# Conditional residual adapter on one core: W1 fetched by id for seventeen batches instead of nine, without the early copy of W1

## The chip, the cores and the metric

The kernel runs on one core of one Trainium2 chip. The metric is the device time of one execution in microseconds (us); of several executions the median is given. A core has five engines that run their own instruction streams in order: TensorE (PE, whose weight loads the profile lists apart as PEld), VectorE (DVE), ScalarE (ACT), GpSimd (POOL) and SyncE (SP), which in this kernel only issues transfers. An instruction starts when the one before it on its engine allows it and the semaphores that it waits for have come.

## The reference: what is computed

There are 128 batches; each has x[b] of 128 rows by 512 columns (256 KB) and an id 0 to 8 that picks one of ten sets of weights.

```
w1 = W1[ids]; w2 = W2[ids]                       # 512x128 and 128x512 for each batch
h = relu(x @ w1 + b1[ids])                       # 128 x 128
y = x + (h @ w2 + b2[ids])                       # 128 x 512
n = (y - mean(y)) * rsqrt(var(y) + 1e-5)         # over the 512 columns
out = x + n * gamma[ids] + beta[ids]
```

All tensors are float32. W1 and W2 of all ten ids are 2560 KB each, x and out are 32 MB each.

## The kernel before, in words

**Per batch.** Each batch goes through the same steps, one batch behind the other on every engine:

- PE: `transpose_x` (line 260, four transposes of x into `pxT`), `down` (line 283, four products of x transposed with the batch's W1 into `ph`, listed as eight passes), `up` (line 300, one product with W2 into `py`, listed as two passes; for batches 0, 1, 126 and 127 a product at line 299 puts b2 there first).
- ACT: `copy_xT` (line 264) copies the transposed x from PSUM, `relu` (line 291), `stage_w1` (line 251) copies the 256 KB of the batch's W1 from the table that holds all ten into a small buffer `w1s`, `square` (line 340) sums squares, and two short steps for mean and deviation.
- POOL: `add_b2` (line 270, `r` = x + b2) and `add_beta` (line 277, `o` = x + beta). For some batches DVE adds b2 instead (line 310).
- DVE: `residual` (line 317), `scale` (line 383), three short steps for 1/deviation, `finish` (line 392, writes the result into `o`).
- SP: `load_x` (line 71, four batches or 1024 KB at a time), `load_part` (line 89, two batches or 512 KB), and `store` (line 396, two batches or 512 KB of `o`).

The function `keep` ties every instruction to the one before it on its engine, so that the order of each engine, SP's queue too, is the order in which the program writes it. `x` has four buffers of four batches; `o` has five buffers of two batches; `w1s` has five buffers of one batch; `py` has five and `pxT` and `ph` one PSUM buffer each. A buffer is filled anew when its last readers are done.

**W1 in the beginning.** For batches 0 to 8 SP loads the batch's own W1 from HBM by its id (`load_first`, line 162, 256 KB; the id is in a register that `lid` at line 144 loads, four ids at a time). Batches 9 to 29 are staged by ACT from `w1e`, a copy of all ten W1 that two loads of 1280 KB bring (`load_early`, line 170). Batches from 30 on are staged from `w1`, the usual copy with its rows in another order, which four loads of 640 KB bring (`load_w1`, line 104) in loop turns 16, 18, 20 and 22. `w1` has 512-byte pieces in HBM; `w1e` and the loads by id have 2 KB pieces, and `transpose_x` takes the columns of x with a stride of four for batches below `EARLY`.

**Opening and loop.** The opening (lines 522 to 561) spreads the rows of beta, gamma and b2 over 128 partitions (`spread` by PE and ACT, `shuffle_rows` at line 236 by DVE) among the first five turns of x; `spin` (line 511) issues idle products. Then a loop over i runs `transpose_x(i)`, `down(i-1)`, `copy_xT(i)`, `relu(i-1)`, `stage_w1(i+1)`, `up(i-2)` and, for b = i - 3, the steps on POOL and DVE; the store of a pair comes when its second batch is finished, first in turn i = 7. The last batches have an order of their own (`tail`).

Of the kernel before, what the change touches and what calls it, by code (L numbers as in the profile page):

```python
# [8 lines left out]
FP = mybir.dt.float32  # L9
# [4 lines left out]
ET = mybir.EngineType  # L14
PSUM = bass.MemoryType.PSUM

P = 128
G = 4
EPS = 1e-5
FIRST = 9  # L20
EARLY = 30
LATE = 12
U = 2


# [1 line left out]
def cond_resid_kernel(ctx: ExitStack, tc: tile.TileContext, x, itok, W1, b1, W2, b2, gamma, beta, out):  # L27
# [8 lines left out]
    nc = tc.nc  # L36
    B, S, H = x.shape
    L, _, A = W1.shape
    KC = H // P
    NG = B // G  # L40
# [5 lines left out]
    def keep(ins):  # L46

        engine = ins.ins.engine
        if engine in last:
            tc.add_manual_dep(ins.ins, last[engine], behind, reason="kept order")  # L50
        last[engine] = ins.ins.name
        return ins

    const = ctx.enter_context(tc.tile_pool(name="const", bufs=1))
    xp = ctx.enter_context(tc.tile_pool(name="xp", bufs=4))
    rp = ctx.enter_context(tc.tile_pool(name="rp", bufs=4))
    op = ctx.enter_context(tc.tile_pool(name="op", bufs=5))
    tp = ctx.enter_context(tc.tile_pool(name="tp", bufs=2))
    wp = ctx.enter_context(tc.tile_pool(name="wp", bufs=5))
    st = ctx.enter_context(tc.tile_pool(name="st", bufs=6))  # L60
    p_x = ctx.enter_context(tc.tile_pool(name="p_x", bufs=1, space=PSUM))
    p_h = ctx.enter_context(tc.tile_pool(name="p_h", bufs=1, space=PSUM))
# [3 lines left out]
    xs = {}  # L66
    E = B - 5

    def load_x(g):
        t = xp.tile([P, G, H], FP, tag="x", name=f"x_{g}")  # L70
        keep(nc.sync.dma_start(out=t, in_=x[g * G : (g + 1) * G].rearrange("b s h -> s b h")))
        xs[g] = t
# [6 lines left out]
    rows = rp.tile([P, H], FP, tag="r", name="rows")  # L79
    b1r = const.tile([L, A], FP, name="b1r")  # L80
    w1 = const.tile([P, L, KC, A], FP, name="w1")
    w1e = const.tile([P, L, KC, A], FP, name="w1e")
    w2 = const.tile([P, L * H], FP, name="w2")
    x_0 = xp.tile([P, G, H], FP, tag="x", name="x_0")
    xs[0] = x_0
# [1 line left out]
    def load_part(lo, hi, engine=nc.sync):  # L87
        dst = xs[lo // G][:, lo % G : lo % G + hi - lo, :]
        keep(engine.dma_start(out=dst, in_=x[lo:hi].rearrange("b s h -> s b h")))  # L89
# [12 lines left out]
    def load_w1(k):  # L102
        keep(
            nc.sync.dma_start(out=w1[:, :, k, :], in_=W1[:, k * P : (k + 1) * P, :].rearrange("l p a -> p l a"))
        )
# [35 lines left out]
    def lid(b, engine):  # L141
        g = b // G
        if (g, engine) not in lids:
            loads, vals = nc.values_load_multi_w_load_instructions(  # L144
                lang[0:1, g * G : (g + 1) * G],
                engines=[engine],
                min_val=0,
                max_val=L - 1,
                skip_runtime_bounds_check_because="clamped on the chip to 0..L-1 above",
            )  # L150
            for ins in loads:
                keep(ins)
            lids[g, engine] = vals
        return lids[g, engine][b % G]
# [4 lines left out]
    def load_first(b):  # L159
        w1s[b] = wp.tile([P, KC, A], FP, tag="w1s", name=f"w1s_{b}")  # L160
        src = W1[bass.ds(lid(b, ET.SP), 1)].rearrange("o (p k) a -> p (o k a)", k=KC)
        keep(nc.sync.dma_start(out=w1s[b].rearrange("p k a -> p (k a)"), in_=src))  # L162
# [2 lines left out]
        dst = w2[:, lo * H : hi * H].rearrange("p (l h) -> p l h", l=hi - lo)  # L165
        keep(nc.sync.dma_start(out=dst, in_=W2[lo:hi].rearrange("l a h -> a l h")))

    def load_early(lo, hi):
        dst = w1e[:, lo:hi].rearrange("p l k a -> p l (k a)")
        keep(nc.sync.dma_start(out=dst, in_=W1[lo:hi].rearrange("l (p k) a -> p l (k a)", k=KC)))  # L170

    load_w2(0, 3)
    load_first(0)
    load_first(1)
# [10 lines left out]
    load_first(7)  # L185
    xs[2] = xp.tile([P, G, H], FP, tag="x", name="x_2")
    load_part(8, 10)
    load_early(0, 5)
    load_first(8)
    load_early(5, L)  # L190
    load_part(10, 12)

    def upper(lo):

# [19 lines left out]
    def spread(r, copier):  # L214
        t = (beta_b, gamma_b, b2_b)[r // L]
        row = p_y.tile([P, H], FP, tag="y", name=f"row_{r}")
        pick_r = pick[:, r : r + 1].to_broadcast([96, P])
        keep(nc.tensor.matmul(row, lhsT=pick_r, rhs=parts[:96, :], start=True, stop=True))
        dst = t[:, r % L * H : (r % L + 1) * H]
        if copier is nc.scalar:  # L220
            keep(nc.scalar.copy(dst, row))
        else:
            keep(nc.vector.tensor_copy(dst, row))
# [9 lines left out]
    def shuffle_rows(lo, hi):  # L233
        for r in range(lo, hi):
            t = (beta_b, gamma_b, b2_b)[r // L]
            keep(nc.vector.stream_shuffle(t[:, r % L * H : (r % L + 1) * H], fours[0], [r] * 32))  # L236
# [10 lines left out]

    def stage_w1(b):
        w1s[b] = wp.tile([P, KC, A], FP, tag="w1s", name=f"w1s_{b}")
        src = (w1e if b < EARLY else w1).rearrange("p l k a -> p (l k a)")[:, bass.ds(lid(b, ET.Activation) * (KC * A), KC * A)]  # L250
        keep(nc.scalar.copy(w1s[b].rearrange("p k a -> p (k a)"), src))  # L251

    def transpose_x(b):
        pxs[b] = p_x.tile([P, KC, P], FP, tag="xT", name=f"pxT_{b}")
        for k in range(KC):
            if b < EARLY:
                cols = xb(b).rearrange("s (p k) -> s k p", k=KC)[:, k, :]
            else:
                cols = xb(b)[:, k * P : (k + 1) * P]
            keep(nc.tensor.transpose(pxs[b][:, k, :], cols, ident))  # L260

    def copy_xT(b):
        xT[b] = tp.tile([P, KC, P], FP, tag="xT", name=f"xT_{b}")
        keep(nc.scalar.copy(xT[b], pxs.pop(b)))  # L264

    def add_b2(b):
        if not b2_by_matmul(b) and not b2_by_vector(b):
            rs[b] = rp.tile([P, H], FP, tag="r", name=f"r_{b}")
            v = lid(b, ET.Pool)
            keep(nc.gpsimd.tensor_tensor(rs[b], xb(b), b2_b[:, bass.ds(v * H, H)], ALU.add))  # L270
# [8 lines left out]
    def down(b):  # L279
        phs[b] = p_h.tile([P, P], FP, tag="h", name=f"ph_{b}")  # L280
        for k in range(KC):
            keep(
                nc.tensor.matmul(  # L283
                    phs[b], lhsT=w1s[b][:, k, :], rhs=xT[b][:, k, :], start=(k == 0), stop=(k == KC - 1)
                )
            )
        del xT[b], w1s[b]

    def relu(b):
        hT[b] = tp.tile([P, P], FP, tag="hT", name=f"hT_{b}", bufs=6)  # L290
        keep(nc.scalar.activation(hT[b], phs.pop(b), AF.Relu, bias=b1T[:, bass.ds(lid(b, ET.Activation), 1)]))  # L291
# [107 lines left out]
    def on(b):  # L399
        return 0 <= b < B  # L400
# [125 lines left out]
    x_turn(0)  # L526
    transpose_b1()
    spread(11, nc.scalar)
    shuffle_rows(0, 10)
    x_turn(1)  # L530
    spread(12, nc.scalar)
# [28 lines left out]
    x_turn(4)  # L560
    up(1)

    for i in range(3, B + U):
        b = i - U - 1
        if b > G and b % G == 2 and b // G + 3 < NG:
            load_x(b // G + 3)
        if i == 5:
            load_x(3)
        if i in (16, 18, 20, 22):
            load_w1((i - 16) // 2)  # L570
        if i > 4 and on(i):
            transpose_x(i)
        if b <= E:
            add_b2(b + 2)
            if 4 <= b + 2 <= E:
                add_beta(b + 2)
        if i > 4 and on(i - 1):
            down(i - 1)
        if i > 4 and on(i):
            copy_xT(i)  # L580
        if i > 4 and on(i - 1):
            relu(i - 1)
        if i + 1 >= LATE and on(i + 1):
            stage_w1(i + 1)
        if i > 3 and on(i - U):
            up(i - U)


        g, half = divmod(b, 2)
        p = g - 1  # L590
        mine, old = 0 <= p < B // 2, 0 <= p - 1 < B // 2
        if b == E:
            add_b2(b + 3)
            add_beta(b + 1)
            add_b2(b + 4)
            for n in range(b + 2, B):
                add_beta(n)
        if b > E:
            tail(b)
        elif half == 0:  # L600
            if on(b):
                vector_b2(b)
                residual(b)
                square(b)
            if mine:
                scale(2 * p)
                rstd(p, 1)
            if old:
                finish(2 * p - 1)
                store(p - 1)  # L610
        else:
            if on(b):
                vector_b2(b)
            if mine:
                rstd(p, 2)
            if on(b):
                residual(b)
                square(b)
            if mine:
                rstd(p, 3)  # L620
                scale(2 * p + 1)
            if mine:
                finish(2 * p)
        if 0 <= g and b <= E and half == 1:
            scalar_means(g)
            deviation(g)
        if FIRST <= i + 1 < LATE:
            stage_w1(i + 1)

        for n, engine in ((i + 3, ET.Activation), (i - U + 3, ET.PE), (b + 1, ET.DVE), (b + 6, ET.Pool)):  # L630
            if on(n):
                lid(n, engine)

# [36 lines left out]
```

## Time and profile before

| what | value |
| --- | --- |
| median of three runs | 306.7 us (306.4 to 306.74) |
| the profiled execution's own time | 306.72 us |
| its span in the profile | 305.0 us |
| PE busy | 292.6 us (96%) |
| DVE busy | 294.4 us (97%) |
| POOL busy | 285.0 us (93%) |
| ACT busy | 282.8 us (93%) |
| moved by DMA | 77.85 MB, mean 255 GB/s |

The span is the time from the first to the last recorded event; 1.7 us of the execution's time lie around it. A busy figure is an average over the opening, the loop and the end, and a matmul's or a POOL instruction's listed length overlaps the next one's, so the distance from one start to the next is the better price of an instruction.

### The profile page before, as it was taken

How to read it: one execution, taken by the hardware profiler on the slowest of the kernel's cores; microseconds unless marked ns; L12 is line 12 of the kernel's file. 1: busy time of each engine (PE TensorE's matmuls, PEld its weight loads, DVE VectorE, ACT ScalarE, POOL GpSimd, SP SyncE). 2: the span in 40 equal slices, each digit the busy share in tenths (PEclk: the TensorE clock that was granted, in tenths of full speed). 3: DMA queues.
4: the chain of work that ended last, by engine and by line, in shares of the span. 5: the costliest groups of instructions: out<-in, count | busy, mean ns of one | idle time of the engine just before them, and what ended most of it. 6: DMA issues, size and time to landing. Idle time of an engine off the chain costs nothing.

```text
span 305.0 us, 6995 instructions
## 1 busy us (share of the span) xinstructions
PE 292.6 (96%) x1821; PEld 220.0 (72%) x1821; DVE 294.4 (97%) x784; ACT 282.8 (93%) x779; POOL 285.0 (93%) x240
## 2 busy tenths in 40 slices
PE   7999899999999999999999999999999999999980
PEld 3858587877777777777777777777777777777740
DVE  5989799999999999999999999999999999999995
ACT  4967899999999999999999999999999999999982
POOL 1199599999999999999999999999999999999995
PEclk9999999999999999999999999999999999999996
DMA  7999996998578766766876666777766766882244
GB/s 233 388 388 386 397 318 187 380 368 315 213 270 277 230 207 224 250 250 222 275 269 214 219 217 253 249 241 275 252 220 205 242 233 234 277 275 103 112 170 172
DMA packets 44057, 77.85 MB, mean 255 GB/s; under 512 B 1993, under 2 KB 7892, under 8 KB 44018
## 3 DMA queue, kind: packets, MB, share of 16 engines
q1 hardware_dynamic: 43382, 76.84, 73.1%
q10 hardware_dynamic: 636, 0.57, 0.6%
q8 instruction: 15, 0.25, 0.3%
q14 instruction: 24, 0.20, 0.2%
HBM read 43.85 MB, written 33.55 MB: 254 GB/s over the span
## 4 chain that ended last, share of the span: by engine, by line
PE 59%; POOL 15%; DMA 8%; issue 8%; DVE 7%; SPq 1%; ACT 1%; POOLq 0%; DVEq 0%; ACTq 0%
PE ph L283 24%; PE py L300 23%; PE pxT L260 12%; POOL o L277 8%; POOL r L270 6%; DMA w1e<-in_L_cond_W_dram 4%; DMA w1s<-in_L_cond_W_dram 3%; DVE py L383 2%; DVE py L317 2%; DVE o L392 1%; DVE py L310 1%; SPq L162 1%; SPq L89 0%; SPq L144 0%; ACT n L439 0%
## 5 line engine op out<-in xcount | busy, mean ns | idle before, releaser
L277 POOL TENSOR_TENSOR o<-x,beta_b 128x512 f32<-128x512 f32 x128 | 172.3, 1381 | 15.3 <-DVE beta_b L236 12.7
L283 PE MATMUL ph<-xT,w1s 128*128 128x128 f32 x1024 | 135.2, 275 | 0.0
L270 POOL TENSOR_TENSOR r<-x,b_b 128x512 f32<-128x512 f32 x97 | 134.1, 1384 | 0.6 <-DMA x<-in_x_dram 0.6
L300 PE MATMUL py<-w,hT 128*128 x256 | 131.3, 595 | 0.0
L283 PEld LDWEIGHTS ph<-xT,w1s 128*128 128x128 f32 x1024 | 125.1, 192 | 1.0 <-ACT hT L291 0.5
L260 PEld LDWEIGHTS pxT<-ident,x 128*128 128x128 f32 x512 | 68.2, 155 | 66.7 <-issue 48.6
L383 DVE SCALAR_TENSOR_TENSOR py<-py,nmean,gamma_b 128x512 f32<-128x512 f32 x126 | 94.8, 752 | 0.0
L392 DVE SCALAR_TENSOR_TENSOR o<-py,rstd,o 128x512 f32<-128x512 f32 x122 | 91.0, 746 | 0.0
L340 ACT ACTIVATE sq<-py,sum 128x512 f32<-128x512 f32 x124 | 85.8, 692 | 0.6 <-DVE py L317 0.6
L260 PE MATMUL pxT<-ident,x 128*128 128x128 f32 x512 | 78.7, 277 | 1.3 <-ACT hT L291 1.3
L264 ACT COPY xT<-pxT 128x512 f32<-128x512 f32 x128 | 74.7, 583 | 3.4 <-PE pxT L260 3.3
L317 DVE SCALAR_TENSOR_TENSOR py<-py,r 128x512 f32<-128x512 f32 x97 | 66.9, 689 | 1.9 <-PE py L300 1.7
L251 ACT COPY w1s<-w 128x512 f32 x98 | 60.0, 613 | 0.0
L291 ACT ACTIVATE hT<-ph,b1T 128x128 f32<-128x128 f32 x128 | 46.9, 367 | 7.0 <-PE ph L283 1.7
L300 PEld LDWEIGHTS py<-w,hT 128*128 128x128 f32 x256 | 39.1, 192 | 1.4 <-issue 0.7
L340 ACT ACTIVATION_READ_ACCUMULATOR sq<-py,sum 128x1 f32 x124 | 25.1, 203 | 0.0
L317 DVE SCALAR_TENSOR_TENSOR py<-py,x 128x512 f32<-128x512 f32 x31 | 21.7, 699 | 1.1 <-PE py L300 0.8
L310 DVE TENSOR_TENSOR py<-py,b_b 128x512 f32<-128x512 f32 x27 | 18.7, 691 | 0.1
L350 ACT ACTIVATE root<-ssq,eps 128x2 f32<-128x2 f32 x62 | 16.5, 265 | 0.0
L251 ACT COPY w1s<-w1e 128x512 f32 x21 | 12.8, 612 | 1.6 <-DMA w1e<-in_L_cond_W_dram 1.6
L317 DVE DVE_READ_ACCUMULATOR py<-py,r 128x1 f32 x97 | 13.5, 139 | 0.0
L331 ACT ACTIVATE nmean<-sum 128x2 f32<-128x2 f32 x62 | 12.3, 198 | 0.0
(58 smaller groups left out, 92.1 us busy)
## 6 DMA issues: line engine op xcount, KB each, us to landing
out_dram<-o SPq DMA_DIRECT2D x61, 512.0 KB, 3.4
x<-in_x_dram SPq DMA_DIRECT2D x29, 1024.0 KB, 6.2
x<-in_x_dram SPq DMA_DIRECT2D x6, 512.0 KB, 8.8
w1e<-in_L_cond_W_dram SPq DMA_DIRECT2D x2, 1280.0 KB, 12.5
w<-in_L_cond_W_dram SPq DMA_DIRECT2D x4, 640.0 KB
w1s<-in_L_cond_W_dram SPq DMA_DIRECT2D x9, 256.0 KB, 8.5
w<-in_L_cond_W_dram SPq DMA_DIRECT2D x1, 1792.0 KB, 10.0
w<-in_L_cond_W_dram SPq DMA_DIRECT2D x1, 768.0 KB, 5.3
```

The costliest lines, as they stand in the source:

```text
L251: keep(nc.scalar.copy(w1s[b].rearrange("p k a -> p (k a)"), src))
L260: keep(nc.tensor.transpose(pxs[b][:, k, :], cols, ident))
L264: keep(nc.scalar.copy(xT[b], pxs.pop(b)))
L270: keep(nc.gpsimd.tensor_tensor(rs[b], xb(b), b2_b[:, bass.ds(v * H, H)], ALU.add))
L277: keep(nc.gpsimd.tensor_tensor(os[g][:, j, :], xb(b), beta_b[:, bass.ds(v * H, H)], ALU.add))
L283: nc.tensor.matmul(phs[b], lhsT=w1s[b][:, k, :], rhs=xT[b][:, k, :], start=(k == 0), stop=(k == KC - 1))
L291: keep(nc.scalar.activation(hT[b], phs.pop(b), AF.Relu, bias=b1T[:, bass.ds(lid(b, ET.Activation), 1)]))
L300: keep(nc.tensor.matmul(ys[b], lhsT=hT[b], rhs=w2[:, bass.ds(v * H, H)], start=not m, stop=True))
L317: nc.vector.scalar_tensor_tensor(ys[b], ys[b], 1.0, r, ALU.mult, ALU.add, accum_out=col(sums, b))
L340: nc.scalar.activation(sq, ys[b], AF.Square, bias=col(sums, b), scale=-float(H), accum_out=col(ssqs, b))
L383: nc.vector.scalar_tensor_tensor(ys[b], ys[b], col(nmeans, b), gamma_b[:, bass.ds(v * H, H)], ALU.add, ALU.mult)
L392: nc.vector.scalar_tensor_tensor(o, ys.pop(b), rstds[g][:, j : j + 1], o, ALU.mult, ALU.add)
```

## The change

The early copy `w1e` and its two loads are gone, and with them ACT's staging for batches 9 to 16. Batches 9 to 16 get their W1 by id as batches 0 to 8 do; ACT stages from `w1` from batch 17 on. The four loads of `w1` and the loads of x for batches 12 to 19 are written into the list ahead of the loop, between the loads by id; so every store stands behind all of these on SP's queue. `o` has eight buffers instead of five, `w1s` seven instead of five. `transpose_x` uses the stride of four up to batch 16 instead of 29. PE loads the ids of batches 0 to 7 into registers ahead of the turn of batch 1 instead of at `up(0)` and in the loop. The loop is written anew around the variable `turned`; the order on each engine that results is the old one, but that `stage_w1` always follows `relu`.

```
-FIRST = 9
-EARLY = 30
-LATE = 12
+FIRST = 17
+EARLY = 17
+LATE = 17
...
-    op = ctx.enter_context(tc.tile_pool(name="op", bufs=5))
+    op = ctx.enter_context(tc.tile_pool(name="op", bufs=8))
...
-    wp = ctx.enter_context(tc.tile_pool(name="wp", bufs=5))
+    wp = ctx.enter_context(tc.tile_pool(name="wp", bufs=7))
...
-    w1e = const.tile([P, L, KC, A], FP, name="w1e")
...
-    def load_early(lo, hi):
-        dst = w1e[:, lo:hi].rearrange("p l k a -> p l (k a)")
-        keep(nc.sync.dma_start(out=dst, in_=W1[lo:hi].rearrange("l (p k) a -> p l (k a)", k=KC)))
...
     load_part(8, 10)
-    load_early(0, 5)
     load_first(8)
-    load_early(5, L)
+    load_first(9)
     load_part(10, 12)
+    load_first(10)
+    load_first(11)
+    xs[3] = xp.tile([P, G, H], FP, tag="x", name="x_3")
+    load_part(12, 14)
+    load_first(12)
+    load_w1(0)
+    load_first(13)
+    load_part(14, 16)
+    load_first(14)
+    load_w1(1)
+    load_first(15)
+    xs[4] = xp.tile([P, G, H], FP, tag="x", name="x_4")
+    load_part(16, 18)
+    load_w1(2)
+    load_first(16)
+    load_part(18, 20)
+    load_w1(3)
...
-        src = (w1e if b < EARLY else w1).rearrange("p l k a -> p (l k a)")[:, bass.ds(lid(b, ET.Activation) * (KC * A), KC * A)]
+        src = w1.rearrange("p l k a -> p (l k a)")[:, bass.ds(lid(b, ET.Activation) * (KC * A), KC * A)]
...
     spread(11, nc.scalar)
+    for n in (0, G):
+        lid(n, ET.PE)
     shuffle_rows(0, 10)
...
+    turned = 5
     for i in range(3, B + U):
         b = i - U - 1
-        if b > G and b % G == 2 and b // G + 3 < NG:
+        if b > G and b % G == 2 and b // G + 3 < NG and b // G + 3 >= 5:
             load_x(b // G + 3)
-        if i == 5:
-            load_x(3)
-        if i in (16, 18, 20, 22):
-            load_w1((i - 16) // 2)
-        if i > 4 and on(i):
-            transpose_x(i)
+        up_to = i
         if b <= E:
+            if turned <= up_to and on(turned):
+                transpose_x(turned)
             add_b2(b + 2)
...
-        if i > 4 and on(i - 1):
-            down(i - 1)
-        if i > 4 and on(i):
-            copy_xT(i)
-        if i > 4 and on(i - 1):
-            relu(i - 1)
-        if i + 1 >= LATE and on(i + 1):
-            stage_w1(i + 1)
-        if i > 3 and on(i - U):
+        for n in range(turned, min(B, up_to) + 1):
+            if on(n) and (n > turned or b > E):
+                transpose_x(n)
+            down(n - 1)
+            if on(n):
+                copy_xT(n)
+            relu(n - 1)
+            if on(n + 1) and n + 1 >= FIRST:
+                stage_w1(n + 1)
+        turned = max(turned, min(B, up_to) + 1)
+        if i - U >= 2 and on(i - U):
             up(i - U)
...
-        if FIRST <= i + 1 < LATE:
-            stage_w1(i + 1)
```

More of the change, by code (lines that the diff above doesn't have):

```diff
@@ L626, in cond_resid_kernel @@
             deviation(g)
-        if FIRST <= i + 1 < LATE:
-            stage_w1(i + 1)
-        for n, engine in ((i + 3, ET.Activation), (i - U + 3, ET.PE), (b + 1, ET.DVE), (b + 6, ET.Pool)):
+        for n, engine in ((turned + 2, ET.Activation), (i - U + 3, ET.PE), (b + 1, ET.DVE), (b + 6, ET.Pool)):
             if on(n):
```

## The prediction

> **What bounds the kernel now.** I read the page for the shares, then the waits of the loop, the waits of the first 60 us, the chain there, and PE's order of time around the gap.
>
> The waits from 60 to 290 us are the whole answer:
>
> ```profile
> PEld pxT L260 <- issue: 42.0, 156, 0.3
> PEld pxT L260 <- ACT xT L264: 12.7, 53, 0.2
> ACT hT L291 <- PE ph L283: 0.7, 3, 0.2
> ```
>
> No engine waits for anything that PE's products do not cover: PE runs end to end. Its turns start 2.22 us apart up to batch 29 (42.23, 44.45, 46.67, ... 75.53) and 2.19 us apart from batch 30 on (77.75, 79.94). DVE, POOL and ACT need nearly as much, so nothing in the loop is to be had but the pace of those first turns. What is lost lies in the opening. Waits from 0 to 60 us (us in total, times, longest):
>
> ```profile
> POOL o L277 <- DVE beta_b L236: 12.7, 1, 12.7
> ...
> POOL o L277 <- DMA out_dram<-o: 2.5, 1, 2.5
> DVE py L317 <- PE py L300: 2.5, 2, 1.7
> ...
> ACT w1s L251 <- DMA w1e<-in_L_cond_W_dram: 1.6, 1, 1.6
> PEld L229 <- DVE parts L199: 1.4, 1, 1.4
> PE pxT L260 <- ACT hT L291: 1.3, 1, 1.3
> ```
>
> The chain there (start, us, what) names the cause: ACT's staging for batch 9 stands in order ahead of its other work and waits for the second half of the early copy.
>
> ```profile
> 18.28 13.49 DMA w1e<-in_L_cond_W_dram
> ...
> 31.85 0.08 ACT w1s L251
> ...
> 32.48 0.48 ACT xT L264
> 32.95 0.28 ACT hT L291
> 33.23 0.03 issue
> 33.26 0.72 PE pxT L260 x4
> ```
>
> PE in order of time shows the only two gaps from 5 us on in the opening (start, length, and in brackets the idle time before):
>
> ```profile
> 17.12 0.38 PE L299 MATMUL py<-parts,pick 96*128 96x512 bf16 x1 [0.55 <-ACT b_b L221]
> ...
> 29.56 0.63 PE L260 MATMUL pxT<-ident,x 128*128 128x128 f32 x4
> ...
> 33.26 0.72 PE L260 MATMUL pxT<-ident,x 128*128 128x128 f32 x4 [1.32 <-ACT hT L291]
> ```
>
> Last, the DMA: 270 GB/s from 0 to 10 us, then 388, 386 and 390 in the next three stretches of ten, with a share of 1.03 to 1.05: a full queue. So the question is what stands in the queue, and when each piece lands.
>
> **The early copy gone.** Turn 10 starts at 33.26; after turn 9 (29.56) the pace would give 31.78. That is 1.48 us on PE, and ACT's wait for w1e, its cause, goes with the copy. What is late next: batch 10's W1 reads w1s of batch 9 by load. Its place in the new queue is 7745 KB (65 of rows, ids and b1, 2560 of x, 2560 of W2, 2560 of ten w1s; 1 KB is 1024 bytes). From the stretches, the queue has moved 10,195 KB by 30.0 us and moves 379 KB per us. A piece lands when some 850 KB beyond its own end have moved: the second half of w1e ended at 10,050 KB and landed at 31.77 (10,870 moved), x of batches 10 and 11 at 10,560 and 33.16 (11,400). So w1s of batch 9 lands near 26.0, against 32.2. ACT also loses eight copies, 8 x 0.51 us from start to start, worth nothing as ACT is not the bound. Gain on PE: 1.5 us. DVE's wait of 1.69 us (before 35.85) and POOL's of 0.55 (for x) and 2.55 us (for the first store, which frees one of five o buffers) go too, so the others can follow: DVE by 1.7, POOL by 3.1.
>
> **Ids ahead of turn 1.** PE's weight load at line 299 stands idle 1.05 us at "issue", and PE 0.55, where the register load (0.33 us each) sits. Two of these now run while PE waits 0.44 us for ACT ahead of turn 1, so turn 1 may start some 0.3 later, and ACT has been busy without a break from there to 17.1. From -0.3 to +0.55 us; I take 0.25, the 0.55 less the 0.3.
>
> **Turns 17 to 29 with contiguous columns.** 13 x (2.22 - 2.19) = 0.4 us. If the others don't follow, 0.
>
> **The loads in front and the stores behind.** This is where the change may lose. The list ends at 65 + 5120 (20 batches of x) + 2560 (W2) + 4352 (17 by id) + 2560 (w1) = 14,657 KB, then the stores. Loads by id 7 to 16 wait for down of batch 0 to 9; with seven buffers load 16 goes at about 33 us, and x, w1 and the first stores are queued behind it on SP. SP also waits for the landing of the eighth DMA before (w1e, its 18th, waited 1.3 us for W2, its 10th). Issued against moved at each such wait: 8513 to some 7200 KB at 22.1, 9281 to 8060 at 24.3, 10,177 to 8900 at 26.5: never under 1200 KB, 3 us of work, so the queue stays full. x of batches 16 and 17 needs the buffer of batches 0 to 3, last read at 24.45 by DVE.
>
> The price of w1's 512-byte pieces is seen in single us, when it came in the loop: into a full queue (57 to 58 us), and into an empty one (50 to 51):
>
> ```profile
> DMA packets 622, 0.35 MB, mean 354 GB/s; under 512 B 5, under 2 KB 597, under 8 KB 622
> ```
>
> ```profile
> DMA packets 415, 0.21 MB, mean 212 GB/s; under 512 B 1, under 2 KB 415, under 8 KB 415
> ```
>
> A part of 655,000 bytes takes 1.69 us at 388 GB/s, 1.86 at 352, 3.36 at 195 (the lowest full us, 49 to 50). Four cost 0.7 us more, or 6.7 at the other end. I take 0.7, as the queue is full. Then:
> - w1's last part lands at 30 + (14,657 + 850 - 10,195)/379 + 0.7 = 44.7. ACT stages batch 17 1.83 us after turn 16 begins (as it did at 37.79 and 39.62): 45.10 - 0.25 + 1.83 = 46.7. Margin 2.0.
> - store 0 lands at 46.1. o of batch 16, the first that needs its buffer, is POOL's 13th from 32.7, 1.235 apart: 47.5. Margin 1.4, with 1.0 of POOL's 3.1 us to spare.
> - x of batches 20 to 23 ends at 17,217 KB behind three stores: 51.5, against turn 20 at 53.7. Margin 2.2. The next x has over 5.
>
> Nothing is late: cost 0, from 0 to 4 us at the low rate.
>
> **Sum.** 1.5 + 0.25 + 0.4 = 2.1 us off the profiled execution's 306.72, which stands at the median: 304.6. The end (tail) moves as it is: DVE's residual of batch 124 starts 0.12 us after PE's up, and POOL comes earlier by more than PE.
>
> **Rivals.**
> *The queue loses its rate* (slower). Place: SP's list from load 11 on, where each load waits for a down. If the queue runs dry there, w1's parts move at the empty queue's 195 GB/s; the last lands at 50.7, 4.0 late; ACT stands, and with it turns 18 on; x of batch 20 is 3.8 late in the same stretch, which is not added. 304.6 + 4.0 = 308.6. It decides from where the lateness eats 2.1: 2.0 + 2.1 us on four parts, a mean part of 2.9 us or 226 GB/s. For it: the rows at 50 us. Against: 352 to 354 in every full us since. A rule of the Trainium skill leans to it (DMA: Bandwidth & Descriptors, section Bandwidth): batch transfers to at least 1 MiB, since each has a fixed cost; here two of 1280 KB become eight of 256 KB. The trace does not agree where transfers queue: from 12 to 14 us, with 256 and 512 KB ones alone, it moved 395 GB/s, against 384 from 26 to 28 with the large ones.
> *Some of it given back*: the parts at some 250 GB/s, or the ids costing 0.3 and one landing 1 us late: 305.5 to 307.0, most of it no more than the measurement can tell.
> *POOL sets the pace*: it works without a break from 37.09 to its last o at 294.87, so its 3.1 us would be the gain: 303.6. Against it: r of batch 125 is ready at 289.75 and read at 293.71.
> That the change isn't done can't be: queue orders are written out.
>
> **Numbers.** Forecast 0.58, range of its own 303.9 to 305.5 (ids -0.3 to +0.55, 0.4 either had or not); rate lost 0.23; partly back 0.14; POOL 0.05. About 0.2% (0.6 us) is what a measurement of this kernel can tell from no change: under 306.1, 0.58 + 0.05 + 0.03 of the third; within, 0.10; over 307.3, 0.24. The range 303.8 to 307.6 leaves out the far half of the first rival and most of POOL's.
>
> **What would show it.** Right: no wait of ACT for w1 or of POOL for a store before 60 us, turn 10 near 31.5, turns at 2.19 from batch 17, no gap on PE between 33 and 60, DMA near 380 GB/s to 50 us. Wrong: a wait of ACT's L251 for w near 46 us, of PE or POOL for x near 54, or the GB/s row dipping under 300 between 22 and 45.

## The result, and the profile after

The changed kernel takes 304.14 us (303.98 to 304.59), the kernel before 306.67: a ratio of 0.9921, 95% interval 0.9904 to 0.9939. That is 2.5 us less, where 2.1 was forecast. The profiled execution took 304.08 us, 2.64 less than that of before, with a span of 302.3.

All lines of the loop have moved down in the code by eleven (`transpose_x` is L271, `down` L294, `up` L311, `stage_w1` L262, `add_beta` L288). The loop's waits from 60 to 290 us (total, times, longest) are nearly what they were (42.0 and 12.7 us before), so no wait was won or lost there:

```profile
PEld pxT L271 <- issue: 42.0, 155, 0.3
PEld pxT L271 <- ACT xT L275: 12.8, 53, 0.4
```

The waits of the first 60 us. Gone are ACT's wait for the early copy and POOL's for x; POOL's wait for a store has shrunk from 2.5 to 1.1 us and is now that of batch 16:

```profile
POOL o L288 <- DVE beta_b L247: 11.6, 1, 11.6
...
POOL o L288 <- DMA out_dram<-o: 1.1, 1, 1.1
DVE py L328 <- PE py L311: 1.1, 1, 1.1
...
PEld pxT L271 <- DMA x<-in_x_dram: 0.8, 1, 0.8
```

The chain there (start, us, what) has no DMA around turn 10: it is PE alone, step behind step.

```profile
29.04 0.47 PE pxT L271 x4
29.50 0.89 PE ph L294 x8
30.40 0.86 PE py L311 x2
31.26 0.47 PE pxT L271 x4
```

PE in order of time: up(0) at 16.15 (17.12 before), turn 9 at 28.87 (29.56), turn 10 at 31.09 without a gap (33.26), and from turn 16 to 17 and 18 the step changes from 2.22 to 2.19 us.

```profile
16.15 0.38 PE L310 MATMUL py<-parts,pick 96*128 96x512 bf16 x1
...
28.87 0.63 PE L271 MATMUL pxT<-ident,x 128*128 128x128 f32 x4
...
31.09 0.63 PE L271 MATMUL pxT<-ident,x 128*128 128x128 f32 x4
...
44.41 0.63 PE L271 MATMUL pxT<-ident,x 128*128 128x128 f32 x4
...
46.63 0.60 PE L271 MATMUL pxT<-ident,x 128*128 128x128 f32 x4
...
48.82 0.60 PE L271 MATMUL pxT<-ident,x 128*128 128x128 f32 x4
```

The rate of w1's 512-byte parts came out worse than forecast. In the two us from 38 to 40 nearly all packets are such pieces (962 of 1023):

```profile
DMA packets 1023, 0.61 MB, mean 305 GB/s; under 512 B 15, under 2 KB 962, under 8 KB 1023
```

One pair of lines bears on a rival that the prediction set aside. POOL in order of time at the end, before and after: the four last steps of `add_beta`, then the first of the closing steps (`n`). Before, `n` follows at once, without a wait of POOL; after, it waits 0.42 us for ACT.

```profile
289.75 5.12 POOL L277 TENSOR_TENSOR o<-x,beta_b 128x512 f32<-128x512 f32 x4
294.75 1.35 POOL L441 TENSOR_TENSOR n<-n,gamma_b 128x512 f32<-128x512 f32 x1
```

```profile
286.55 5.14 POOL L288 TENSOR_TENSOR o<-x,beta_b 128x512 f32<-128x512 f32 x4
292.11 1.27 POOL L452 TENSOR_TENSOR n<-n,gamma_b 128x512 f32<-128x512 f32 x1 [0.42 <-ACT n L450]
```

The page's chain that ended last (shares of the span by engine), before and after, says the same. Before, POOL holds 15% of it beside PE's 59%; after, it holds none.

```profile
PE 59%; POOL 15%; DMA 8%; issue 8%; DVE 7%; SPq 1%; ACT 1%; POOLq 0%; DVEq 0%; ACTq 0%
```

```profile
PE 89%; DVE 5%; DMA 2%; issue 1%; ACT 1%; SPq 0%; POOL 0%; DVEq 0%; ACTq 0%; POOLq 0%
```

### The profile page after: what moved, and what is told of

The parts are those of the page before. It is cut to its first block, busy times and chain, and to the rows that moved or that the text cites. A ratio compares the mean times of both kernels' runs of the same rounds, so it can differ in the third digit from the quotient of the medians.

```text
span 302.3 us, 7001 instructions
## 1 busy us (share of the span) xinstructions
PE 290.6 (96%) x1820; PEld 218.0 (72%) x1821; DVE 294.2 (97%) x784; ACT 279.6 (92%) x771; POOL 284.9 (94%) x240
## 4 chain that ended last, share of the span: by engine, by line
PE 89%; DVE 5%; DMA 2%; issue 1%; ACT 1%; SPq 0%; POOL 0%; DVEq 0%; ACTq 0%; POOLq 0%
PE ph L294 36%; PE py L311 35%; PE pxT L271 18%; DMA x<-in_x_dram 2%; DVE py L394 2%; DVE py L328 1%; DVE o L403 1%; PE row L229 1%; SPq L161 0%; ACT n L450 0%; ACT sq L351 0%; ACT sq L436 0%; DVE o L461 0%; ACT w1s L262 0%; DVE rstd L370 0%
## 5 line engine op out<-in xcount | busy, mean ns | idle before, releaser
L288 POOL TENSOR_TENSOR o<-x,beta_b 128x512 f32<-128x512 f32 x128 | 170.1, 1359 | 12.7 <-DVE beta_b L247 11.6
L294 PE MATMUL ph<-xT,w1s 128*128 128x128 f32 x1024 | 135.3, 275 | 0.2 <-DMA w1s<-in_L_cond_W_dram 0.2
L281 POOL TENSOR_TENSOR r<-x,b_b 128x512 f32<-128x512 f32 x97 | 131.7, 1360 | 0.0
L311 PE MATMUL py<-w,hT 128*128 x256 | 131.3, 595 | 0.0
L294 PEld LDWEIGHTS ph<-xT,w1s 128*128 128x128 f32 x1024 | 124.8, 192 | 1.3 <-issue 0.6
L271 PEld LDWEIGHTS pxT<-ident,x 128*128 128x128 f32 x512 | 66.0, 149 | 66.8 <-issue 49.9
L271 PE MATMUL pxT<-ident,x 128*128 128x128 f32 x512 | 77.6, 274 | 0.8 <-DMA x<-in_x_dram 0.6
L262 ACT COPY w1s<-w 128x512 f32 x111 | 68.0, 613 | 0.0
L311 PEld LDWEIGHTS py<-w,hT 128*128 128x128 f32 x256 | 39.1, 192 | 1.4 <-issue 0.7
L365 DVE SCALAR_TENSOR_TENSOR part<-ssq,root 128x2 f32<-128x2 f32 x62 | 9.3, 149 | 0.2 <-ACT root L361 0.2
```

Source lines behind the costliest of these rows:

```text
L288: keep(nc.gpsimd.tensor_tensor(os[g][:, j, :], xb(b), beta_b[:, bass.ds(v * H, H)], ALU.add))
L294: nc.tensor.matmul(phs[b], lhsT=w1s[b][:, k, :], rhs=xT[b][:, k, :], start=(k == 0), stop=(k == KC - 1))
L311: keep(nc.tensor.matmul(ys[b], lhsT=hT[b], rhs=w2[:, bass.ds(v * H, H)], start=not m, stop=True))
```

## The experiments

**e1: the ids alone, on the kernel before.**

```
     spread(11, nc.scalar)
+    for n in (0, G):
+        lid(n, ET.PE)
     shuffle_rows(0, 10)
```

> The kernel before with one part of the change alone: PE loads the ids of batches 0 to 7 ahead of turn 1. In the profiles, up(0) starts 0.97 us sooner after the change (16.15 against 17.12) and turn 5 0.69 sooner, where 0.25 was forecast. Theory A (the register load of 0.33 us stood on PE's path ahead of up(0), 0.55 us of idle): 306.7 - 0.4 to 0.6, so 306.1 to 306.3, if POOL's late start does not eat it. Theory B (PE's first products ran at the half pace in the profile of before, a 512-column product each 0.43 us against 0.22, and at the full pace in the profile of after; this differs from run to run of the same program): 306.7 within 0.2, and here or in other runs the opening shows either pace with either kernel. Theory C (turn 5 sooner, but batch 10 still waits for x of batches 10 and 11 and for the early copy, which land at the same time as before): turn 10 at 33.2 and 306.6.

Measured: 306.73 us, ratio 0.9999 (0.999 to 1.0008). PE in order of time:

```profile
28.94 0.63 PE L260 MATMUL pxT<-ident,x 128*128 128x128 f32 x4
...
33.12 0.72 PE L260 MATMUL pxT<-ident,x 128*128 128x128 f32 x4 [1.80 <-ACT hT L291]
```

and POOL:

```profile
33.12 1.28 POOL L270 TENSOR_TENSOR r<-x,b_b 128x512 f32<-128x512 f32 x1 [1.50 <-DMA x<-in_x_dram]
36.98 1.28 POOL L277 TENSOR_TENSOR o<-x,beta_b 128x512 f32<-128x512 f32 x1 [2.57 <-DMA out_dram<-o]
```

Turn 9 comes 0.62 us sooner than before (28.94 against 29.56), turn 10 only 0.14 (33.12 against 33.26). The gain is given back at the old gap. POOL's r of batch 10 starts in the same 0.01 us as turn 10, and it waits for x alone: x of batches 10 and 11 lands then, just as in the kernel before (POOL 33.26, PE 33.26). Theory C. The chain that ended last shows how little POOL had to spare in this kernel: with PE sooner by a little (turn 127 at 290.53 instead of 290.66), it lies on POOL for 54% of the span and on PE for 2%.

```profile
POOL 54%; issue 22%; DVE 8%; DMA 8%; POOLq 3%; PE 2%; SPq 1%; ACT 1%; DVEq 0%; ACTq 0%
```

**e2: the changed kernel without the ids ahead.** The diff is the two added lines of e1 taken out.

> The changed kernel without that part: ids of batches 0 to 7 loaded where they were. Theory A: turn 5 0.4 to 0.6 us later, 304.14 + 0.5 = 304.6. Theory B: 304.1 to 304.3. Up(0) shows the idle of 0.55 us and the register load again in both; theory B has the difference in the clock of the first 8 us.

Measured: 304.77 us (304.67 to 305.07), ratio 0.9933 (0.9919 to 0.9947): 0.6 us over the changed kernel, or 0.4 if each is taken by its ratio to the kernel before that was measured beside it (0.9933 less 0.9921). The two intervals overlap, so the time alone does not show it. PE:

```profile
7.75 1.13 PE L271 MATMUL pxT<-ident,x 128*128 128x128 f32 x4
...
17.20 0.38 PE L310 MATMUL py<-parts,pick 96*128 96x512 bf16 x1 [0.55 <-ACT hT L302]
...
20.76 0.63 PE L271 MATMUL pxT<-ident,x 128*128 128x128 f32 x4
```

The idle 0.55 us ahead of up(0) is back and turn 5 starts at 20.76 (19.99 in the changed kernel). Whether theory A or B holds was left to e3, which had the same half-pace first products.

**e3: stride of four kept up to batch 29.**

```
-            if b < EARLY:
+            if b < 30:
```

> The changed kernel with the stride of four kept in the transposes up to batch 29 (for batches 17 to 29 x's columns then do not go with W1's rows, so those outputs differ; the time is what is looked at). Theory: turns 17 to 29 at 2.22 us instead of 2.19, 13 x 0.03 = 0.39 us, 304.5. Rival: another engine (ACT at 2.10 a batch, POOL at 2.19) hides it: 304.1.

Measured: 304.72 us (304.5 to 304.85), ratio 0.9931 (0.9917 to 0.9945). Turn 127 starts at 288.44, 0.42 us later than the 288.02 of the changed kernel; the turns are 2.22 apart up to batch 29. The theory's 0.39 us is on the path. The time rose by 0.58, or by 0.3 by the ratios (0.9931 less 0.9921); the step between the turns shows the term better than the time does. Its opening also bears on theory B:

```profile
7.75 1.13 PE L271 MATMUL pxT<-ident,x 128*128 128x128 f32 x4
...
16.42 0.38 PE L310 MATMUL py<-parts,pick 96*128 96x512 bf16 x1
...
20.01 0.63 PE L271 MATMUL pxT<-ident,x 128*128 128x128 f32 x4
```

Turn 1 starts at 7.75 here and in e2, with the first products at half pace in both, but up(0) at 16.42 against 17.20 and turn 5 at 20.01 against 20.76. So a difference is left that the pace does not make. The stretch from turn 3 to up(0) gives its size: it takes 3.97 to 3.98 us in all nine profiles with the register loads ahead, at either pace, and 4.59 to 4.60 in the three without (the kernel before, e2, e6). The register loads are worth 0.62 us there. How much of it reaches turn 5 differs: PE's weight load then waits for x of batch 4 (0.83 us in the changed kernel, 0.45 here), and in e5, e9 and e10, with the loads ahead and at half pace too, turn 5 starts at 20.33 to 20.43. So theory A holds, and part of B: either pace comes with the same program, and it may move turn 5 by up to 0.4 us.

**e4: seven output buffers instead of eight.**

```
-    op = ctx.enter_context(tc.tile_pool(name="op", bufs=8))
+    op = ctx.enter_context(tc.tile_pool(name="op", bufs=7))
```

> The changed kernel with seven output buffers instead of eight: o of batch 14 instead of batch 16 waits for store 0, which landed at 47.4. Theory P (POOL has next to nothing to spare: the first o that waits is at 41.5 in the profile of after, so 5.9 us of wait instead of 1.1, and at the end POOL waited only 0.42 us for ACT): 304.1 + 4.4 = 308.5. Rival Q (only PE sets the end, POOL's wait is hidden behind its lead): 304.1 to 304.5.

Measured: 307.64 us, ratio to the kernel before 1.0029 (1.0017 to 1.0042): slower than before. POOL:

```profile
47.31 1.27 POOL L288 TENSOR_TENSOR o<-x,beta_b 128x512 f32<-128x512 f32 x1 [5.78 <-DMA out_dram<-o]
```

4.7 us more of waiting made the kernel 3.5 us slower; POOL's first closing step moved from 292.11 to 296.22, 4.1 later. Theory P, 0.9 too high. From 285 us to the end the chain that ended last is POOL's alone. One buffer less costs more than the whole change brings.

**e5: five w1s buffers instead of seven.**

```
-    wp = ctx.enter_context(tc.tile_pool(name="wp", bufs=7))
+    wp = ctx.enter_context(tc.tile_pool(name="wp", bufs=5))
```

> The changed kernel with five w1s buffers instead of seven: loads by id 9 to 16 wait for down of batch 4 to 11, two turns (4.4 us) later than with seven. Theory R (the rival of the prediction: the queue runs dry at each such wait and loses its rate): the last part of w1 lands 3 to 5 us later than the 45.6 or so of the changed kernel, ACT waits for it at batch 17, POOL waits for store 0 some 5 us instead of 1.1, and the time is 307 to 309. Theory D (two turns are covered by what is queued, 1200 KB or 3 us and more): no wait of PE over 0.5 us, 304.1 to 304.6.

Measured: 305.85 us, ratio 0.9961 (0.9946 to 0.9977), 1.7 over the changed kernel. DMA by stretches (stretch, us, granted clock, DMA share, GB/s), first e5, then the changed kernel:

```profile
22.00:26.00 4.00, 1.00 0.78 263
26.00:30.00 4.00, 1.00 0.95 294
```

```profile
22.00:26.00 4.00, 1.00 1.04 383
26.00:30.00 4.00, 1.00 1.09 352
```

The queue did run dry: a share of 0.78 and 263 GB/s against 1.04 and 383. What comes of it is theory R's sign at half its size. ACT in order of time, `relu` and then the staging of batch 17:

```profile
46.32 0.37 ACT L302 ACTIVATE hT<-ph,b1T 128x128 f32<-128x128 f32 x1 [0.31 <-PE ph L294]
48.32 0.62 ACT L262 COPY w1s<-w 128x512 f32 x1 [1.64 <-DMA w<-in_L_cond_W_dram]
```

ACT waits 1.64 us for w1, PE stands 1.16 us behind it ahead of turn 18, POOL waits 2.35 us for store 0. (Turn 5 already came 0.34 us later than in the changed kernel, at the slower pace of the first products.)

**e6: the kernel before with three more batches by id.**

```
-FIRST = 9
+FIRST = 12
...
-    wp = ctx.enter_context(tc.tile_pool(name="wp", bufs=5))
+    wp = ctx.enter_context(tc.tile_pool(name="wp", bufs=6))
...
     load_first(8)
-    load_early(5, L)
+    load_first(9)
     load_part(10, 12)
+    load_first(10)
+    load_first(11)
+    load_early(5, L)
...
-    sq = tp.tile([P, H], FP, tag="sq", name=f"sq_{b}")
+    sq = tp.tile([P, H], FP, tag="sq", name=f"sq_{b}", bufs=1)
```

The last line stands for both places where `sq` is made.

> The kernel before with three more batches (9, 10, 11) by id and x of batches 10 and 11 ahead of the second half of the early copy, six w1s buffers (the squares' scrap tile has one buffer instead of two to make room), five output buffers, all else as before. Turn 10 should start at 31.8 instead of 33.26, as the wait for the early copy and for x are both gone; store 0 has 768 KB more ahead of it and lands 2 us later, so POOL's o of batch 10 waits some 4.5 us instead of 2.55. Theory P (POOL sets the pace in the kernel before as much as PE): no gain, 306.8 + 1 to 2 us. Theory Q (PE's turn 10 is the whole gain): 306.8 - 1.4 = 305.4.

Measured: 307.67 us, ratio 1.0031 (1.002 to 1.0043). PE, then POOL:

```profile
31.83 0.63 PE L263 MATMUL pxT<-ident,x 128*128 128x128 f32 x4
...
38.08 0.72 PE L263 MATMUL pxT<-ident,x 128*128 128x128 f32 x4 [1.65 <-DMA x<-in_x_dram]
```

```profile
39.30 1.27 POOL L280 TENSOR_TENSOR o<-x,beta_b 128x512 f32<-128x512 f32 x1 [5.35 <-DMA out_dram<-o]
```

Turn 10 starts at 31.83 as expected, and then turn 12 waits 1.65 us for the next x: the copy's bytes are still in the queue, only behind other pieces, and the load of this x was issued at 25.70 us, against 22.17 in the kernel before. POOL's wait for store 0 grew to 5.35 us. PE's turn 127 comes at 291.05, 0.39 later than before, POOL's closing step at 296.93, 2.2 later; the time is 0.9 up. As PE lost its gain again at turn 12, the run is no clean test of P against Q; but the time rose by more than PE's 0.39, and from 287.10 us to the end the chain that ended last is POOL's.

**e7: w1's parts in 2 KB pieces.**

```
-            nc.sync.dma_start(out=w1[:, :, k, :], in_=W1[:, k * P : (k + 1) * P, :].rearrange("l p a -> p l a"))
+            nc.sync.dma_start(
+                out=w1[:, (0, 3, 5, 8)[k] : (3, 5, 8, 10)[k]].rearrange("p l k a -> p l (k a)"),
+                in_=W1[(0, 3, 5, 8)[k] : (3, 5, 8, 10)[k]].rearrange("l (p k) a -> p l (k a)", k=KC),
+            )
```

> The changed kernel with w1's four parts in 2 KB pieces instead of 512-byte ones (3, 2, 3 and 2 ids each; W1's rows then do not go with x's columns from batch 17 on, so those outputs differ; the time is what is looked at). In the profile of after the 512-byte parts moved at 305 to 320 GB/s in a full queue where 352 was forecast. Theory: GB/s stay at 385 from 28 to 44 us, store 0 lands some 2 us sooner, POOL's wait of 1.1 us for it goes, and the time stays at 304.1 within 0.2, as PE sets the pace and POOL had 0.4 us over at the end. Rival (POOL or the queue still sets it): 303.0 to 303.6.

Measured: 304.26 us (304.14 to 304.37), ratio 0.9917 (0.9904 to 0.9931): the same as the changed kernel. DMA from 38 to 40 us, then POOL at the end:

```profile
DMA packets 409, 0.77 MB, mean 387 GB/s; under 512 B 31, under 2 KB 31, under 8 KB 409
```

```profile
292.16 1.27 POOL L455 TENSOR_TENSOR n<-n,gamma_b 128x512 f32<-128x512 f32 x1 [1.68 <-ACT n L453]
```

The rate is 387 GB/s instead of 305, no wait of POOL for a store is left, and all of its 1.1 us turns into waiting at the end: 1.68 us instead of 0.42. Neither the parts' rate nor POOL sets the changed kernel's pace; PE does.

**e8: up(1) ahead of the turn of batch 4, nine output buffers.**

```
     up(0)
-    x_turn(4)
     up(1)
+    x_turn(4)
...
-    op = ctx.enter_context(tc.tile_pool(name="op", bufs=8))
+    op = ctx.enter_context(tc.tile_pool(name="op", bufs=9))
```

> The changed kernel with up(1) ahead of the turn of batch 4 in the opening, and nine output buffers. In the profile of after, PE's weight load waited 0.8 us for x of batch 4 at 17.5 while up(1) was ready. Theory: turn 5 starts 0.35 us sooner, POOL's wait for store 0 goes, 303.8. Rival (DVE's shuffles end at 18.5 and hold the first residuals, or batch 5's turn is held by ACT): 304.1.

Measured: 304.14 us, ratio 0.9916 (0.9902 to 0.9929): no gain. PE, then ACT:

```profile
18.60 0.63 PE L271 MATMUL pxT<-ident,x 128*128 128x128 f32 x4
...
19.96 0.74 PE L271 MATMUL pxT<-ident,x 128*128 128x128 f32 x4
```

```profile
19.32 0.58 ACT L275 COPY xT<-pxT 128x512 f32<-128x512 f32 x1 [2.33 <-PE pxT L271]
```

Turn 4 moved to 18.60, ACT copies its result from 19.32 on, and turn 5, which needs the one `pxT` buffer, starts at 19.96, where it was. The rival, in its second form.

**e9: x of batches 10 and 11 late in the list, all else as changed.**

```
     load_first(9)
-    load_part(10, 12)
...
     load_w1(0)
+    load_part(10, 12)
     load_first(13)
```

> The changed kernel with x of batches 10 and 11 put later in the list, behind the first part of w1, so that it lands near 33, as it did in the kernel before (33.16); W1 of batch 9 stays early. Theory X (in the kernel before x alone would have held turn 10; the early copy's bytes ahead of it are the cause, not only ACT's wait for the copy): turn 10 starts at 32.5 to 33.5 instead of 31.09, POOL's r of batch 10 at the same time, and the time rises by 1.4 to 2.4 us, to 305.5 to 306.5. Theory W (ACT's staging alone held it): turn 10 near 31.1 and 304.1.

Measured: 305.82 us, ratio 0.9971 (0.9958 to 0.9983), 1.7 over the changed kernel.

```profile
29.31 0.63 PE L271 MATMUL pxT<-ident,x 128*128 128x128 f32 x4
...
32.43 0.72 PE L271 MATMUL pxT<-ident,x 128*128 128x128 f32 x4 [0.73 <-DMA x<-in_x_dram]
```

Turn 10 waits for x and nothing else, 3.12 us after turn 9 instead of 2.22: 0.90 us of the loss. Another 0.44 was there at turn 9, from this profile's opening at the slower pace. POOL's r of batch 10 comes at 32.64, without a wait. Theory X: x alone can hold turn 10.

**e10: w1's parts at the place of the early copy.**

```
     load_part(8, 10)
+    load_w1(0)
+    load_w1(1)
     load_first(8)
+    load_w1(2)
+    load_w1(3)
     load_first(9)
...
-    load_w1(0)
...
-    load_w1(1)
...
-    load_w1(2)
...
-    load_w1(3)
```

> The changed kernel with the four parts of w1 put at the place in the list where the early copy stood, around the load of batch 8's W1, instead of among the last loads by id: the same 2560 KB ahead of W1 of batch 9 and x of batch 10 as in the kernel before, but nothing staged by ACT before batch 17. Theory X (what counts is the bytes ahead of what PE needs next): x of batches 10 and 11 lands at 35 to 38 (the parts move at some 315 GB/s), turn 10 starts then instead of at 31.09, and the time is 308 to 311, slower than the kernel before. Theory W (ACT's staging was the cause): 304.1 to 304.6.

Measured: 310.53 us, ratio 1.0124 (1.0107 to 1.0141).

```profile
35.89 1.10 PE L271 MATMUL pxT<-ident,x 128*128 128x128 f32 x4 [4.29 <-DMA x<-in_x_dram]
36.78 1.91 PE L294 MATMUL ph<-xT,w1s 128*128 128x128 f32 x8
```

Turn 10 starts at 35.89, held by x. The same number of bytes as the early copy's, at the same place, with no staging by ACT before batch 17, costs more than the early copy did; these come in 512-byte pieces, which move more slowly. Theory X again, and W falls.

## Why the prediction was right, point by point

- **The bound.** Right for the changed kernel: PE's turns, 2.22 and 2.19 us, are the pace, and the opening was where time was lost. Turn 127 moved by 2.64 us (290.66 to 288.02), the profiled time by as much. For the kernel before it was half the truth, as POOL bounded it too (see the rivals below).
- **The early copy, 1.5 us.** Right in size: turn 10 is 2.17 us sooner, of which 0.69 came with turn 5; 1.48 is left. The cause was told too narrowly. The prediction named ACT's wait for w1e as the cause and x's landing at 33.16 only as a datum for its queue; e1 shows PE and POOL released together when x lands, e9 that x alone holds turn 10, e10 that staging isn't needed for the loss. The two were late together, since x stood behind the same 2560 KB whose end ACT waited for. `relu`, the releaser that the lines name, is inferred: by the program turn 10 needs x and, of ACT, `copy_xT` of batch 9, and that copy ended at 32.95 in the kernel before. So ACT's wait by itself may have cost some 0.3 us less than x's, which no run here shows. Loading batches 9 to 11 by id and x of 10 and 11 sooner, with the copy's bytes still there (e6), only moved the gap to turn 12.
- **The ids, 0.25 us.** The term that was mis-sized: 0.69 at turn 5 in the first two profiles, 0.4 to 0.6 in time by e2. The step that failed is the 0.3 taken off for a later turn 1. Both loads fit into PE's wait for ACT there: turn 1 starts at 7.75 with them (e3) and without (e2). From turn 3 to up(0) 0.62 us is won, and what of it is left at turn 5 varies: 0.25 to 0.75 us between the profiles at half pace. That the forecast of 2.1 fell short of 2.5 is mostly this term's doing.
- **Turns 17 to 29, 0.4 us.** Right: 0.42 at turn 127 by e3.
- **The loads in front.** The queue stayed full from 22 to 46 us as worked out, and none of these loads came late for PE or ACT. The price of w1's parts was too low: 305 to 320 GB/s in the two-us stretches that were nearly all such pieces, where 352 was taken. That 352 is from 52 to 54 us, where 512 of 731 packets were small; the 354 shown had 597 of 622, and why it was higher stays open. It is also not so that every full us since had 352 to 354: 61 to 62 us moved 336, 62 to 63 us 333. So store 0 landed at 47.4 instead of 46.1, POOL came for its buffer at 46.4 instead of 47.5, and waited 1.1 us where none was forecast. Of the prediction's signs of being right two did not come: this wait, and a rate near 380 GB/s to 50 us (it was 305 to 365 from 28 to 44). It cost nothing (e7), but only just.
- **The rivals.** The queue running dry is real: e5 brings it about with two buffers less, at 1.7 us. It did not happen with seven. One row against this rival was misread: from 12 to 14 us the queue did not move 256 and 512 KB loads alone. By the sizes in the list the bytes from 2881 to 4673 KB are W2's larger part, one load of 1792 KB that was issued at 6.24 and landed at 16.2; some 3370 to 4140 KB had moved by the start and the end of that stretch. The changed kernel's 383 GB/s from 22 to 26 us is a row that shows it. "POOL sets the pace" was set aside for a wrong reason: r of batch 125 was early, but the order on POOL puts four steps of `add_beta` behind it, and `n` followed these without a wait. By the shares of the chain (PE 59% and POOL 15% before, 2% and 54% in e1) the two bounded that kernel together; the gain needed POOL's waits gone too, and e4 shows that seven output buffers turn the change into a loss of 0.3%.

## What to carry to other kernels

When a piece lands late, list what stands ahead of it in the queue and ask of each byte when it is first needed; a bulk copy whose first use is one tile may be replaced by loads of the tiles, as here. When stores move behind loads, count output buffers until the first store's landing, and when engines are balanced, look at each one's last free moment at the end of the kernel, not only at its waits, before calling it hidden. Register loads that an engine needs later can go into a wait that it has anyway, where they cost nothing here.

## What the runs showed of the hardware

- TensorE's first products ran at two paces in otherwise equal openings. A 512-column product starting at 4.78 us took 0.58 to 0.59 us in the profiles of before, e2, e3, e5, e6, e9 and e10, 0.38 to 0.40 in those of the changed kernel, e1, e4 and e7, and 0.48 in e8, while the granted clock read 1.00 in the kernels before and after. It moved POOL's first step (13.09 to 13.17 against 14.16 to 14.19) and turn 5 by less (with the register loads ahead, 19.96 to 20.05 against 20.01 to 20.43). The Trainium skill (TensorE: Matmul & The Clock Gate, section Part 1: The HAM clock gate) says that the window in which the clock is released runs freely and does not start with the kernel, which agrees with a pace that changes from run to run.
- After the idle 4.29 us in e10 the products ran at half pace, eight passes of `down` in 1.91 us instead of 1.06, and there the granted clock shows it (stretch, us, PE busy, granted clock, DMA share, GB/s):

```profile
36.00:38.00 2.00, 2.00 (x10) 0.50 1.05 395
```

  The same section of the Trainium skill gives half rate after an idle window of some 3.4 us. This case agrees as far as it goes: half pace after 4.29 us, full pace after 1.80 us (e1, `down` in 1.06). It is an extra price of a long wait: turn 11 came 3.89 us after turn 10.
- 512-byte pieces in a full queue moved 305 GB/s, 2 KB pieces 387, in the same two us of otherwise equal kernels (the changed one and e7). Loads of 256 and 512 KB in 2 KB pieces kept 383 from 22 to 26 us in the changed kernel, against 384 from 26 to 28 with the 1280 KB ones in the kernel before, so their size cost nothing here.
- What stays open: how much more the opening can give. W2's larger part lands at 16.03 (issued at 6.23, 9.8 us to landing), 0.1 us ahead of up(0), and e8 found the next holder, ACT's copy of the single `pxT` buffer; neither was changed.
